# Layer 0's PSUM rings, two filters on TensorE, and placed transposes in a kernel of six stages

## The chip, the core and the metric

The kernel runs on one core of one Trainium2 chip, in one launch. The metric is the device time of that launch in microseconds: the median of several runs, lower is better. The profile is one further execution, taken by the hardware profiler, with a span of its own.

## What is computed

A batch of 8 images of 256 channels and 32 x 32 pixels goes through four layers; all numbers are fp32. The change touches the first layer, the feed-forward of the third, and the start of the fourth:

```python
# layer 0: attention of 4 heads, then a gated convolutional feed-forward
a = _attention(_ln(x, norm1_w, norm1_b), ...)     # _ln: x * rsqrt(mean(x*x)) * w + b
x = x + gamma1 * a
f = _edffn(_ln(x, norm2_w, norm2_b), ...)
x = x + gamma2 * f
# _attention: q, k, v by 1x1 convolution and batch norm; softmax(q k) v; plus a 3x3
#   depthwise convolution of v (pe); then a projection with batch norm (proj)
# _edffn: 1x1 convolution to 1024 channels (pi), 3x3 depthwise convolution,
#   gelu(first 512) * last 512, 1x1 convolution back (po), and in each 8x8 patch
#   a Fourier transform, a gain for each frequency, and the inverse
# layer 1: deformable convolution with group norms
# layer 2: causal attention with an MLP, then a feed-forward of the better half of the tokens
idx = top_k(x @ wr + br)[:, :511]; sel = x[idx]
y = (gelu(sel @ w1 + b1) @ w2 + b2) * weight[idx]
x = x + scatter(y, idx)
# layer 3: attention with squared scores on 8 heads, then a mixture of 8 experts
t = t + attention(layer_norm(t)); t = t + moe(layer_norm(t))
```

## The kernel before

The program is written in stages (`fast0`, `fast1`, `fast2`, `fast2f`, `fast3`, `fast3e`), each a Python generator that records instructions. Between two yields lies a piece of work. `by_time` (L1077) draws pieces from several such streams by their due times, so that pieces of different samples interleave. A scheduler then orders the instructions of each engine, within the data dependences, and may move one past its neighbours; `net.pinned` (L1037) keeps an instruction at the place in which it was recorded, relative to the other pinned ones of its engine. Every engine then executes its list strictly in order: an instruction that waits holds up all behind it. The tail of a stage overlaps the head of the next (`net.head`).

Tiles come from pools. A pool with n buffers hands them out in rotation, and a new tile waits until all readers of the one n places before it are done. [...]

**Layer 0** (`fast0`, L1094). The stream `attention` makes 128 steps: for each sample, each half of 512 queries (gq), and each of 8 key tiles (kt). A step makes the scores `s` of four heads (L1357, in two pairs of banks), their exponentials `e` on ScalarE (L1363), and, for the step before, sums of e on VectorE (L1319) and the products with v, which accumulate in `A` (L1323, one pair of banks of its own). After the eighth key tile `finish` normalises (D, rr, av, o) and projects (`proj`, L78, with the sum on VectorE in L1351). T = 32 ticks belong to one sample. Beside it run, each at due times of its own:

- `before_attention`: the norm (`ms`, `rb`, L1219), q, k and v (`qkv`), transposes of v (`vT`), the 3x3 convolution of v (`pe`, L1290).
- `before_gates` and `gates`: the second norm; for each of 8 groups of 128 channels the 1x1 convolution (`pi`, evacuated to `hp` in L1398), and then `depthwise`: the centre tap on ScalarE (L1223) and eight taps as one VectorE instruction each (L1230).
- `transforms`: `po`, the Fourier transform forward into the second bank of the same pair (L1455), the gain (L1456), the inverse (`back`, L1463), and the residual sum on VectorE (L1469).

All PSUM tiles but A come from one pool, `psS`, with three buffers of two banks: scores and all else take turns in it, and what needs one bank takes the first of a pair. When the 128 steps are recorded, `att.close()` frees the attention's space, and the rest of layer 0 goes on beside the head of layer 1.

**Layer 2's feed-forward** (`fast2f`, L2004). For each sample `before` ranks the tokens, `place` scatters the chosen ones to DRAM, `ready` loads them (xs), transposes them on TensorE (L2137) and copies them to `xk` on VectorE (L2138), `main` makes the two matrix products (h: L78, y: L2155), `after` gathers the results back (POOL) and adds them to the stream of tokens (L2182). T = 13 ticks belong to a sample.

**Layer 3** (`fast3`, L2457). `norm` loads a sample (SP's queue), normalises its tokens on VectorE (L1002, L1014), adds the output's bias to x on POOL (L2508), and transposes the result (L2514, copied in L2515).

Of the kernel before, what the change touches and what calls it, by code (L numbers as in the profile page):

```python
# [10 lines left out]
F32 = mybir.dt.float32  # L11
# [7 lines left out]
B = 8  # L19
# [1074 lines left out]
def fast0(net, io):  # L1094
# [3 lines left out]
    NT = N // P  # L1098
    yield HOLD
    with ExitStack() as ctx, ExitStack() as att:  # L1100
# [4 lines left out]
        psS = io.pool(ctx, "f0s", 3, PSUM)  # L1105
# [5 lines left out]
        psA = io.pool(att, "f0am", 1, PSUM)  # L1111
# [24 lines left out]
        def pair(name):  # L1136
            return psS.tile([P, 2, HF], F32, tag="S", name=name)

        def bank(name):
            return pair(name)[:, 0]  # L1140
# [51 lines left out]
        def sc(i):  # L1192
            return s[:, i : i + 1]
# [4 lines left out]
        def normed(xn, x, sq):  # L1198
# [13 lines left out]
            pr = pair("rb")  # L1212
            for h in range(2):
                nc.tensor.matmul(
                    pr[:, h], lhsT=net.unit[64 * h : 64 * h + 1, :], rhs=r[64 * h : 64 * h + 1, :],
                    start=True, stop=True,
                )
            pr = pr.rearrange("p h n -> p (h n)").unsqueeze(1).to_broadcast([P, KC, N])
            nc.vector.tensor_tensor(xn, x, pr, ALU.mult)  # L1219
# [13 lines left out]

        def before_attention(b):
# [6 lines left out]
            def projected(d, w, j, norm):  # L1241
                ps = pair("qkv")
                for h in range(2):
                    net.linear(ps[:, h], w, xn, bass.ts(j, P), bass.ts(h, HF))
                nc.scalar.activation(d, ps.rearrange("p h n -> p (h n)"), AF.Identity, scale=sc(norm), bias=sh(norm))
# [10 lines left out]
            for t4 in range(0, NT, 4):  # L1256
                ps = pair("vT")
                for i in range(4):
                    for c in range(KC):
                        lo = (i % 2) * C + c * P  # L1260
                        nc.tensor.transpose(ps[:, i // 2, lo : lo + P], v[:, c, bass.ts(t4 + i, P)], net.ident)
                nc.scalar.copy(
                    va[:, t4 : t4 + 4].rearrange("p t c d -> p (t c d)"), ps.rearrange("p h n -> p (h n)")
                )
                yield

            o = os[b] = atwo.tile([P, KC, N], F32, tag="o", name="o")
            for c in range(KC):
                ps = pair("pe")
                for h in range(2):  # L1270
# [12 lines left out]
                    yield  # L1283
                    for j, s_ in enumerate((0, -1, 1)):
                        for g in range(4):
                            to, fr = (
                                img(a)[:, :, max(0, -d_) : IMG - max(0, d_)]
                                for a, d_ in ((ps[32 * g : 32 * g + 32, h], s_), (thrice[:, g, :], -s_))
# [3 lines left out]
                            )  # L1292
                    yield
                nc.scalar.activation(
                    o[:, c, :], ps.rearrange("p h n -> p (h n)"), AF.Identity, scale=sc(4 + c), bias=sh(4 + c)
                )
                yield

        def attention():
# [31 lines left out]
            def finish(b, gq, A, total, x):  # L1331
# [16 lines left out]
                ps = pair("proj")  # L1348
                for c in range(KC):
                    net.linear(ps[:, c], wproj, o, bass.ts(c, P), cols)  # L1350
                    nc.vector.scalar_tensor_tensor(x[:, c], ps[:, c], sh(6 + c), x[:, c], ALU.add, ALU.add)  # L1351
                nc.sync.dma_start(out=mids[b][:, :, cols], in_=x)

            for i, (b, gq, kt) in enumerate(steps):
                ss = [pair("s") for _ in range(2)]
# [34 lines left out]
        def gates(b):  # L1390
            xn = xs.pop(b)

            def convolved(i):
                hp = two.tile([P, N], F32, tag="hp", name="hp")
                ps = pair("pi")
                for h in range(2):
                    net.linear(ps[:, h], wpi, xn, bass.ts(i, P), bass.ts(h, HF))
                nc.scalar.activation(hp, ps.rearrange("p h n -> p (h n)"), AF.Identity, bias=pib[:, i : i + 1])  # L1398
                a = cv[i] = five.tile([P, N], F32, tag="a", name="a")
                yield  # L1400
                yield from depthwise(img(a), img(hp), lambda t_: dw_taps[:, i, t_ : t_ + 1])
# [26 lines left out]
        def transforms(b):  # L1428
# [12 lines left out]
            for pr in range(4):  # L1441
# [3 lines left out]
                ps = pair("po")  # L1445
                for pc in range(2):
                    for k in range(4):
                        nc.tensor.matmul(
                            ps[:, 0, bass.ts(pc, C)], lhsT=hc[:, k, pc, :], rhs=wpo[:, k, :],
# [1715 lines left out]
```

## Time and profile before

| | us |
|---|---|
| median of 3 runs | 4487.3 |
| lowest and highest run | 4487.09, 4494.2 |
| the profiled execution | 4425.21 |
| its span, first to last instruction | 4423.1 |
| granted TensorE clock, mean | 0.953 |

By stretches of the span (busy us of each engine; the last column is the clock that TensorE was granted, as a share of full speed):

| stretch, us | what runs | PE | DVE | ACT | clock |
|---|---|---|---|---|---|
| 0 to 110.6 | layer 0 starts | 89.2 | 26.7 | 36.9 | 0.95 |
| 774.2 to 884.8 | layer 0, attention beside the feed-forward | 101.6 | 86.3 | 51.9 | 0.98 |
| 1327.2 to 1437.8 | layer 0 without attention, head of layer 1 | 79.5 | 94.5 | 41.0 | 0.87 |
| 1659.0 to 1769.6 | layer 1 | 102.1 | 87.7 | 71.7 | 1.00 |
| 2101.4 to 2212.0 | layer 2, attention | 108.5 | 31.7 | 43.0 | 1.00 |
| 2765.0 to 2875.6 | layer 2, feed-forward | 100.9 | 81.6 | 58.7 | 0.95 |
| 2875.6 to 2986.2 | its end and the start of layer 3 | 88.5 | 33.9 | 20.1 | 0.89 |
| 3428.6 to 3539.2 | layer 3, attention | 109.3 | 24.8 | 63.7 | 1.00 |
| 4202.8 to 4313.4 | layer 3, experts | 94.3 | 54.1 | 53.0 | 0.95 |

How to read profile rows in this text: a group has its line, engine and operation, then out<-in with shapes, then how often it ran, busy us and the mean ns of one, then the engine's idle time before it and who ended that. A wait is written as waiter <- releaser. A row of the timeline has a start, a duration, the instruction, how many of them, and in brackets the idle time before. TensorE shows two rows for one fp32 matmul, so x8 of pi are four matmuls. PE is TensorE's matmuls, PEld its weight loads, DVE VectorE, ACT ScalarE, POOL GpSimd, SP SyncE.

### The profile page before, as it was taken

How to read it: one execution, taken by the hardware profiler on the slowest of the kernel's cores; microseconds unless marked ns; L12 is line 12 of the kernel's file. 1: busy time of each engine (PE TensorE's matmuls, PEld its weight loads, DVE VectorE, ACT ScalarE, POOL GpSimd, SP SyncE). 2: the span in 40 equal slices, each digit the busy share in tenths (PEclk: the TensorE clock that was granted, in tenths of full speed). 3: DMA queues.
4: the chain of work that ended last, by engine and by line, in shares of the span. 5: the costliest groups of instructions: out<-in, count | busy, mean ns of one | idle time of the engine just before them, and what ended most of it. 6: DMA issues, size and time to landing. Idle time of an engine off the chain costs nothing. (4 is left out here: it accounts for less than half of the span.)

```text
span 4423.1 us, 52368 instructions
## 1 busy us (share of the span) xinstructions
PE 4007.3 (91%) x19836; PEld 1905.5 (43%) x19836; DVE 2321.2 (52%) x3976; ACT 2140.6 (48%) x2730; POOL 556.3 (13%) x633
## 2 busy tenths in 40 slices
PE   8989999999887889989999969988999999999887
PEld 3223333333333444444444436653333433336776
DVE  2387777777888677742222257732233223324345
ACT  3454445445443466633334355515555555566443
POOL 0000000000000000000000023420000000353753
PEclk9999999999998899999999979989999999999998
DMA  2212222222222111010001023371100000245667
GB/s 86 81 47 83 86 74 88 81 79 79 73 89 77 61 59 50 31 41 19 20 19 39 10 75 107 121 222 51 34 30 29 14 16 30 75 125 197 186 216 253
DMA packets 188423, 348.44 MB, mean 79 GB/s; under 512 B 23706, under 2 KB 132460, under 8 KB 176644
## 3 DMA queue, kind: packets, MB, share of 16 engines
q1 hardware_dynamic: 165396, 293.31, 20.5%
q0 software_dynamic: 19104, 46.45, 3.1%
q10 hardware_dynamic: 3664, 5.24, 0.3%
q8 instruction: 160, 2.62, 0.2%
q14 instruction: 99, 0.81, 0.1%
HBM read 174.24 MB, written 152.04 MB: 74 GB/s over the span
## 5 line engine op out<-in xcount | busy, mean ns | idle before, releaser
L1230 DVE SCALAR_TENSOR_TENSOR a<-hp,w_f_vec,a 128x992 f32<-128x992 f32 (+1 forms) x512 | 627.9, 1232 | 145.9 <-ACT a L1223 138.3
L2626 ACT ACTIVATE e<-s,five 128x1024 f32<-128x1024 f32 x512 | 539.5, 1109 | 280.5 <-PE s L2620 279.1
L2620 PE MATMUL s<-q,k 32*128 32x512 f32 x2048 | 371.2, 678 | 20.4 <-ACT e L2626 18.3
L1363 ACT ACTIVATE e<-s 128x1024 f32<-128x1024 f32 x256 | 249.6, 1019 | 228.7 <-PE s L1357 228.6
L2604 PE MATMUL A<-e,v 128*32 128x512 f32 x2048 | 297.3, 634 | 17.1 <-ACT e L2626 17.1
L1319 DVE TENSOR_TENSOR sum<-sum,e 128x1024 f32<-128x1024 f32 x192 | 230.8, 1220 | 114.8 <-ACT e L1363 114.8
L1323 PE MATMUL A<-e,va 128*32 128x512 f32 x2048 | 290.8, 605 | 0.0
L78 PE MATMUL pi<-xn,w_l_wpi 128*128 128x512 f32 x512 | 243.7, 619 | 36.7 <-ACT e L1363 20.0
L1357 PE MATMUL s<-q,k 32*128 32x512 f32 x1024 | 193.5, 642 | 12.8 <-DVE xn L1219 7.1
L2620 PEld LDWEIGHTS s<-q,k 32*128 32x128 f32 x2048 | 117.4, 192 | 201.5 <-issue 86.6
L1398 ACT ACTIVATE hp<-pi,pib 128x1024 f32<-128x1024 f32 x64 | 71.3, 1114 | 230.8 <-PE pi L78 222.5
L78 PEld LDWEIGHTS pi<-xn,w_l_wpi 128*128 128x128 f32 x512 | 96.0, 196 | 175.0 <-issue 108.6
L1681 PE MATMUL pos<-pos,w_f_sel 64*128 64x512 f32 x576 | 161.9, 627 | 7.7 <-ACT ay L1703 3.3
L2774 PE MATMUL h<-xk,w 128*128 128x128 f32 x1136 | 143.7, 281 | 20.4 <-DVE xk L2762 20.4
L1021 POOL DMA_INDIRECT res<-y,to x142 | 143.0, 1007 | 121.1 <-issue 84.7
L2745 ACT COPY w<-w_l3f_w 128x512 f32 x142 | 88.1, 623 | 143.2 <-PE h L2774 140.8
L2774 PEld LDWEIGHTS h<-xk,w 128*128 128x128 f32 x1136 | 140.4, 196 | 27.0 <-DVE xk L2762 20.4
L78 PE MATMUL h<-xk,w_l2f_w 128*128 128x512 f32 x256 | 124.3, 648 | 27.7 <-DVE xk L2138 27.7
L1274 POOL MEMSET thrice<- 32x128 f32 x32 | 6.3, 196 | 1109.7 <-PE pe L1290 1109.7
L1323 PEld LDWEIGHTS A<-e,va 128*32 128x32 f32 x2048 | 61.6, 110 | 194.1 <-issue 191.5
L2604 PEld LDWEIGHTS A<-e,v 128*32 128x32 f32 x2048 | 42.5, 110 | 236.6 <-issue 203.9
L1021 POOL DMA_INDIRECT so<-xl,rows x128 | 129.4, 1011 | 88.9 <-DMA xl<-mox 60.9
(396 smaller groups left out, 7031.0 us busy)
## 6 DMA issues: line engine op xcount, KB each, us to landing
x<-d SPq DMA_DIRECT2D x32, 1024.0 KB
xs<-so SPq DMA_DIRECT2D x70, 260.0 KB
so<-zero SPq DMA_DIRECT2D x5, 3380.0 KB
thrice<-v SPq DMA_DIRECT2D x256, 64.0 KB
gated<-st SPq DMA_DIRECT2D x32, 512.0 KB
hc<-gated SPq DMA_DIRECT2D x32, 512.0 KB
d<-x SPq DMA_DIRECT2D x16, 1024.0 KB
xl<-mox SPq DMA_DIRECT2D x64, 256.0 KB
```

The costliest lines, as they stand in the source:

```text
L78: self.nc.tensor.matmul(ps, lhsT=w[:, i, m], rhs=src[:, i, cols], start=(i == 0), stop=(i == k - 1))
L1021: made = self.nc.gpsimd.indirect_dma_start(**args)
L1230: nc.vector.scalar_tensor_tensor(to, fr, taps(t_), to, ALU.mult, ALU.add)
L1319: nc.vector.tensor_tensor(half, half, e[j], ALU.add)
L1323: nc.tensor.matmul(state["A"][32 * h : 32 * h + 32, c, :], lhsT=vas[b][:, kt, c, 32 * h : 32 * h + 32], rhs=e[h // 2][:, h % 2, :], start= ...
L1357: nc.tensor.matmul(ss[h // 2][:, h % 2], lhsT=ks[b][32 * h : 32 * h + 32, bass.ts(kt, P)], rhs=qs[b][32 * h : 32 * h + 32, bass.ts(gq, HF) ...
L1363: nc.scalar.activation(es[i][j], ss[j], AF.Exp, scale=SCALE)
L1681: nc.tensor.matmul(ps[:, bass.ts(h, HF)], lhsT=sel[r, t, xy, :], rhs=poss[b][r, :], start=True, stop=True)
L2604: nc.tensor.matmul(A[32 * h : 32 * h + 32], lhsT=v[:, kt, c * P + 32 * h : c * P + 32 * h + 32], rhs=e[:, h, :], start=first, stop=last,)
L2620: nc.tensor.matmul(ss[h // 2][:, h % 2], lhsT=k[32 * h : 32 * h + 32, c, bass.ts(kt, P)], rhs=q[32 * h : 32 * h + 32, c, bass.ts(hh, HF)], ...
L2626: nc.scalar.activation(e[:, 2 * j : 2 * j + 2], ss[j], AF.Square, scale=SCALE, bias=five)
L2774: nc.tensor.matmul(ps[:, j, m], lhsT=ws[j][:, k, bass.ts(m, P)], rhs=xk[:, j, k], start=(k == 0), stop=(k == KC - 1),)
```

## The change

1. **Layer 0, PSUM.** Scores get a pool of two pairs of their own. Everything else takes single banks from a pool of two ("X"). What was evacuated as one pair is now evacuated bank by bank (v, q, k, hp, vT, pe). The projection's result goes to av through ScalarE with its bias, and VectorE adds it to x from SBUF; `back` goes to u through ScalarE in the same way. The norm's product with rb is made in two halves. `finish` has one more yield before the projection.
2. **Layer 0, last sample.** Channel groups 1 and 7 are convolved by `by_products`: nine diagonal matrices made on ScalarE, and nine matmuls for each half image that accumulate in one bank, copied out by ScalarE. From the end of attention on, X is a pool of four banks.
3. **Layer 2, feed-forward.** The first transpose of xs of each sample, and the first matmul of each group of y, are pinned. `ready` is due at 8.8 instead of 9, with 1.9 instead of 2.2 between its pieces. For the last two samples the sums of `after` are due at T(b + 2) + 5 instead of + 1.2.
4. **Layer 3, norm.** The first sample is loaded by ScalarE's queue, the others by SP's as before. The bias on POOL is recorded after the transposes instead of before them.

```diff
-        psS = io.pool(ctx, "f0s", 3, PSUM)
+        own = {"X": io.pool(ctx, "f0x", 2, PSUM)}
...
-        psA = io.pool(att, "f0am", 1, PSUM)
+        psS, psA = io.pool(att, "f0s", 2, PSUM), io.pool(att, "f0am", 1, PSUM)
...
-        def pair(name):
-            return psS.tile([P, 2, HF], F32, tag="S", name=name)
-
         def bank(name):
-            return pair(name)[:, 0]
+            return own["X"].tile([P, HF], F32, tag="X", name=name)
...
-            pr = pair("rb")
             for h in range(2):
+                pr = bank("rb")
                 nc.tensor.matmul(
...
+                cols = bass.ts(h, HF)
+                nc.vector.tensor_tensor(
+                    xn[:, :, cols], x[:, :, cols], pr.unsqueeze(1).to_broadcast([P, KC, HF]), ALU.mult
+                )
...
+        def by_products(out, src, i):
+
+            diag = own["diag"].tile([P, 9, P], F32, tag="dg", name="dg")
+            for t_ in range(9):
+                nc.scalar.activation(diag[:, t_], net.ident, AF.Identity, scale=dw_taps[:, i, t_ : t_ + 1])
+            for h in range(2):
+                ps = bank("dw")
+                for n, t_ in enumerate((4, 0, 1, 2, 3, 5, 6, 7, 8)):
...
+                    nc.tensor.matmul(
+                        img(ps)[:, lo - HROWS * h : hi - HROWS * h, x0:x1], lhsT=diag[:, t_],
+                        rhs=img(src)[:, lo + dy : hi + dy, x0 + dx : x1 + dx], start=(n == 0), stop=(n == 8),
+                    )
+                    if n in (4, 8):
+                        yield
+                nc.scalar.copy(out[:, bass.ts(h, HF)], ps)
...
             def projected(d, w, j, norm):
-                ps = pair("qkv")
                 for h in range(2):
-                    net.linear(ps[:, h], w, xn, bass.ts(j, P), bass.ts(h, HF))
-                nc.scalar.activation(d, ps.rearrange("p h n -> p (h n)"), AF.Identity, scale=sc(norm), bias=sh(norm))
+                    ps = bank("qkv")
+                    net.linear(ps, w, xn, bass.ts(j, P), bass.ts(h, HF))
+                    nc.scalar.activation(d[:, bass.ts(h, HF)], ps, AF.Identity, scale=sc(norm), bias=sh(norm))
...
-                ps = pair("proj")
+                yield
                 for c in range(KC):
-                    net.linear(ps[:, c], wproj, o, bass.ts(c, P), cols)
-                    nc.vector.scalar_tensor_tensor(x[:, c], ps[:, c], sh(6 + c), x[:, c], ALU.add, ALU.add)
+                    ps = bank("proj")
+                    net.linear(ps, wproj, o, bass.ts(c, P), cols)
+                    nc.scalar.activation(av[:, c], ps, AF.Identity, bias=sh(6 + c))
+                nc.vector.tensor_tensor(x, x, av, ALU.add)
...
-                ss = [pair("s") for _ in range(2)]
+                ss = [psS.tile([P, 2, HF], F32, tag="S", name="s") for _ in range(2)]
...
-                yield from depthwise(img(a), img(hp), lambda t_: dw_taps[:, i, t_ : t_ + 1])
+                if b == B - 1 and i in BY_PRODUCTS:
+                    yield from by_products(a, hp, i)
+                else:
+                    yield from depthwise(img(a), img(hp), lambda t_: dw_taps[:, i, t_ : t_ + 1])
...
-                nc.tensor.matmul(ps[:, 1], lhsT=fwd, rhs=u.rearrange("p t c -> p (t c)"), start=True, stop=True)
+                ps = bank("fwd")
+                nc.tensor.matmul(ps, lhsT=fwd, rhs=u.rearrange("p t c -> p (t c)"), start=True, stop=True)
...
+                nc.scalar.copy(u.rearrange("p t c -> p (t c)"), back)
                 for c in range(KC):
                     xt = x[:, c, :].rearrange("p (h q w) -> p q h w", q=2, w=16)
-                    nc.vector.tensor_tensor(
-                        xt, back[:, 0, bass.ts(c, C)].rearrange("p (q h w) -> p q h w", q=2, w=16), xt, ALU.add
-                    )
+                    nc.vector.tensor_tensor(xt, u[:, c].rearrange("p (q h w) -> p q h w", q=2, w=16), xt, ALU.add)
...
         att.close()
+        own["X"], own["diag"] = io.pool(ctx, "f0t", 4, PSUM), io.pool(ctx, "f0d", 2)
...
-                    nc.tensor.transpose(ps[:, c * S + t * P : c * S + (t + 1) * P], xs[:, t, bass.ts(c, P)], net.ident)
+                    made = nc.tensor.transpose(
+                        ps[:, c * S + t * P : c * S + (t + 1) * P], xs[:, t, bass.ts(c, P)], net.ident
+                    )
+                    if c + t == 0:
+                        net.pinned(made)
...
-                        nc.tensor.matmul(
+                        made = nc.tensor.matmul(
                             ps[:, bass.ts(i, C)], lhsT=hid[:, k, bass.ts(t2 + i, P)], rhs=w2[:, k, :],
                             start=(k == 0), stop=(k == H // P - 1),
                         )
+                        if k == 0:
+                            net.pinned(made)
...
-                (T * (b - 1) + 9, 2.2, ready(b)), (T * b, 1, main(b) if b < B - 1 else last),
+                (T * (b - 1) + 8.8, 1.9, ready(b)), (T * b, 1, main(b) if b < B - 1 else last),
...
-            streams += [(T * (b + 1) + 7.6, 0.6, some(gathers, NT)), (T * (b + 2) + 1.2, 1, gathers)]
+            streams += [(T * (b + 1) + 7.6, 0.6, some(gathers, NT)), (T * (b + 2) + (1.2 if b < B - 2 else 5), 1, gathers)]
...
-            nc.sync.dma_start(out=halves(x), in_=tokens(io.src[b]))
+
+            (nc.sync if b else nc.scalar).dma_start(out=halves(x), in_=tokens(io.src[b]))
             yield
             xt = one.tile([P, NT, C], F32, tag="xt", name="xt")
             net.token_norm(xt, x, norms)
-            nc.gpsimd.tensor_tensor(x, x, bo.unsqueeze(1).to_broadcast([P, NT, C]), ALU.add)
             yield
...
+            nc.gpsimd.tensor_tensor(x, x, bo.unsqueeze(1).to_broadcast([P, NT, C]), ALU.add)
```

## The prediction

> **What bounds the kernel now.** I read the page first, then the waits of TensorE in layer 0, then busy times by stage, then the order of time at two seams. Rows of the page:
>
> ```profile
> span 4423.1 us, 52368 instructions
> ...
> PE 4007.3 (91%) x19836; PEld 1905.5 (43%) x19836; DVE 2321.2 (52%) x3976; ACT 2140.6 (48%) x2730; POOL 556.3 (13%) x633
> ...
> L1230 DVE SCALAR_TENSOR_TENSOR a<-hp,w_f_vec,a 128x992 f32<-128x992 f32 (+1 forms) x512 | 627.9, 1232 | 145.9 <-ACT a L1223 138.3
> ```
>
> TensorE is busy 91% of the span, so only what shortens its waits, or a stretch in which another engine rules, can move the end. The depthwise taps (L1230) are VectorE's largest group. From 221 to 1327 us (the attention loop of layer 0; ten windows of 110.6 us, added up) PE is busy 1005 of 1106 us, DVE 879, ACT 523. So PE leads, DVE follows at 79%, and ACT is half free. What PE waits for in layer 0 (us in total, times, longest):
>
> ```profile
> PE pi L78 <- ACT e L1363: 20.0, 18, 1.1
> PE proj L78 <- DVE x L1351: 15.8, 11, 2.5
> PE pi L78 <- DVE xn L1219: 13.4, 7, 2.3
> PE proj L78 <- DVE o L1346: 12.7, 3, 7.1
> PE qkv L78 <- DVE xc L1469: 9.3, 4, 2.3
> PE proj L78 <- ACT e L1363: 7.8, 7, 1.1
> ...
> PE s L1357 <- DVE xn L1219: 7.1, 5, 5.7
> ```
>
> Most of these are no data: pi does not use e, qkv does not use xc, s does not use xn. They are waits for a slot of the one ring of three bank pairs that scores and everything else share. The slot is held by an exponential, or by a sum on VectorE that stands behind depthwise taps of 1.23 us.
>
> After the loop VectorE rules. The stages (busy PE, PEld, DVE, ACT, POOL, then granted clock):
>
> ```profile
> 1420.00:1456.00 36.00, 6.66 (x26) 3.40 (x29) 35.87 (x45) 11.10 (x15) 0.00 (x0) 0.68 0.14 49
> ...
> 1302.00:1456.00 154.00, 96.70 (x318) 44.89 (x314) 128.96 (x146) 51.21 (x66) 6.01 (x6) 0.81 0.26 94
> ```
>
> At the end of layer 0 DVE is solid and PE waits 13.16, 7.97 and 4.87 us for layer 1's group statistics, queued on DVE among taps.
>
> Layer 2's feed-forward repeats this once per sample (start, duration, idle before):
>
> ```profile
> 2746.18 1.04 PE L2137 MATMUL xs<-ident,xs 128*128 128x128 f32 x8
> 2747.05 1.04 PE L2046 MATMUL xT<-ident,x 128*128 128x128 f32 x8
> 2750.82 15.39 PE L78 MATMUL h<-xk,w_l2f_w 128*128 128x512 f32 x32 [2.73 <-DVE xk L2138]
> ```
>
> and at the seam to layer 3 stand
>
> ```profile
> 2903.97 13.98 PE L2155 MATMUL y<-w_l2f_w,hid 128*128 128x256 f32 x64
> 2930.74 3.92 PE L2514 MATMUL xn<-ident,xt 128*128 128x128 f32 x16 [12.80 <-DVE xt L1014]
> 2934.70 1.13 PE L78 MATMUL qk<-xn,w_l_wq 128*128 128x512 f32 x2
> 2941.69 7.80 PE L78 MATMUL qk<-xn,w_l_wq 128*128 128x512 f32 x14 [5.86 <-DVE xn L2515]
> ```
>
> ```profile
> 2917.98 0.69 DVE L2160 TENSOR_TENSOR y<-y,w_f_b 128x512 f32<-128x512 f32 x1 [6.21 <-PE y L2155]
> ...
> 2926.05 0.75 DVE L1002 BATCH_NORM_STATS2 tn_s<-x 128x6 f32<-128x256 f32 x2 [6.55 <-DMA x<-d]
> ```
>
> **1. The rings of PSUM in layer 0.** Scores get two pairs of their own; all else gets two single banks, which ScalarE empties except for the normalising rows (rb) and the product with gain (fwd).
> Removed: waits for a slot held by ScalarE, 20.0 + 7.8 and four small rows (2.9, 2.2, 1.6, 1.1) = 35.6 us; held by VectorE, 15.8 + 9.3 + 7.1 and 1.5, 1.2, 0.5 = 35.4 us. The additional pause before proj gives the sums on DVE (o, 12.7) time: about 6 more. Together 77 us.
> Added on ACT: a 128x1024 eviction splits in two. Rows: hp 1.114 us for 1024 columns, hid (L2147) 0.687 for 512, so 0.26 us more for each of 128 splits, 33 us; 32 evictions of proj at 0.69 = 22; 32 of back at 0.585 (the row of u) = 19. These 74 us lift ACT from 47% to about 56% of the loop. [...]
> DVE: proj 32 x 0.747 becomes 16 x 1.22 (4.4 less), rb 16 x 2.28 becomes 32 x 1.22 (2.5 more): nothing.
> New waits: two banks turn about 448 times. In the built order, the PE work (from the trace's durations) between the last matmul into a bank and its next user is 1.9 us or more nearly everywhere, against 0.69 for an eviction plus at most 1.02 for an exponential ahead of it. The short ones: six times none (transposes of v right behind the mean square, which must wait for its logarithm: 0.69 and half an exponential, say 1.5 each, 9 us); five times 1.0 (2 us); fifteen behind rb, where DVE must multiply, 1.22 plus its queue. Most of those stand today as pi and qkv <- xn (13.4 + 4.7), so 4 us more. For the 60-odd places with 1.9, 0.2 each: 12. Together 27 us; behind a waiting matmul stand the next scores, so such a wait is paid in full. Bounds: 5 (only the certain ones) to 77 (0.17 per turn, nothing won). I take 27, since the distances nearly always exceed the eviction. **Net 50.**
>
> **2. Two depthwise filters of the last sample on TensorE.** DVE loses 16 taps x 1.23 = 19.7 us. PE gains 36 matmuls, two rows each, at 0.45 (pi x8 takes 3.60 us in this stretch), a little less at the edges: 31 us. ACT: 18 diagonals of 128x128 (hid L2780: 0.367) = 6.6 us. PE then has 97 + 31 = 128 us of work in 154, DVE 109. Bounds: 19.7 gained if PE hides everything; below, PE's 128 plus about 21 us of short waits that stay = 149, 5 gained. Second cost: on ACT's queue the diagonals stand before the loads of layer 1's weights, and PE already waits 4.9 us for one of those; up to 8 us more, taking 5 to -3. [...] **Net 10.**
>
> **3. Transposes in the feed-forward.** In the built order the eight xs transposes now stand before the last eight y matmuls (3.62 us) rather than directly before h. Today xk is ready 0.87 + 2.73 = 3.6 us after them, so the wait is just covered. Six waits (2.73 three times, 2.41, 2.55, 3.41) plus 0.57 = 17.1. Both xT groups now come before y, which covers most of the 0.2 to 0.5 us before wrow: 1. The first wait (10.6) stays. VectorE does xk at once, ahead of the ranking; the second y sum falls behind it, and the third h waits for its bank, some 1 us later than that sum ends, so nothing. Bounds: 9 to 19. **Net 18.**
>
> **4. The seam to layer 3.** The first x load goes to ACT's queue, behind the last gelu and a table load (ends 2906.2), instead of SP's, behind the store of y that waits until 2918.7. That load took up to 7.4 us then, so it lands near 2913. The statistics then wait for the last y sum, not for it: about 2919.8 instead of 2926.05 (6.2). The eight s sums (5.94 us) between the two xn copies go behind them: 5.86 shrinks to about 1 (5). The later sums and gathers wait on nobody near. The bias add stays first in POOL's order. Bounds 4 to 14. **Net 11.**
>
> **Sum.** 50 + 10 + 18 + 11 = 89. The profiled execution took 4425.2 us, so it would take 4336. The timed runs of before stand 1.4% above it; I take 89 from their median 4487.3: **4398**.
>
> **Rivals.**
> - *Two banks are too few, gain eaten* (part 1 nil): 39 gained, 4448. For: six turns with no work between. Against: the other distances.
> - *Two banks choke PE* (slower): every bank waits behind two exponentials. It decides above (77 + 39) / 448 = 0.26 us per turn; at 0.4 it costs 179, so 4487 - 116 + 179 = 4550. For: ACT serves scores and banks in one order. Against: exponentials are 2 us in steps of about 10.
> - *The tail becomes TensorE's*: part 2 loses 6, 4414. For: 128 of 154.
> - *xk comes no earlier in time* although it stands earlier: part 3 nil, 4416. Against: DVE waits for wrow just then.
> - *More falls than the slots*: the remaining waits on xn, u and o (some 30 us) go too, 4368.
>
> **Numbers.** Chances: forecast 0.62, too few 0.12, tail 0.09, xk 0.04, more 0.09, choke 0.04. All low ends of 1 to 4 together gain 0 - 3 + 9 + 4 = 10 us (4477), all high ends 72 + 20 + 19 + 14 = 125 (4362); all low ends at once are unlikely, so the range is 4355 to 4452, which takes in every rival but the slower one. 0.2% is about what this measurement can tell: faster 0.95, same 0.01, slower 0.04.
>
> **What would show it.** pi and proj no longer wait for e or x of DVE, and PE's share in the loop rises above 94%; vT waits for the logarithm; 16 fewer taps and PE over 125 us busy between loop and layer 1; h without 2.7 us waits; xn at the seam waits about 6.6 us, qk about 1. Wrong if PE gets new waits on bank evictions of over 50 us, or if DVE in the loop goes above 90%.

## The result, and the profile after

| | before | after |
|---|---|---|
| median of 6 runs, us | 4487.6 | 4449.5 |
| lowest and highest | 4470.8, 4499.7 | 4440.6, 4465.0 |
| ratio, 95% interval | | 0.9919 [0.9892, 0.9946] |
| the profiled execution, us | 4425.2 | 4449.3 |

The change gains 38 us where 89 were forecast. The two profiled executions can't be subtracted from one another: that of before took less time than any of its timed runs (4471 us and more), that of after is like its own. A second profile of before, taken later, serves below where stages are compared.

The page of the changed kernel begins with its span, then busy time, share and instructions by engine. The third row is the group of the depthwise taps:

```profile
span 4447.6 us, 52740 instructions
...
PE 4051.6 (91%) x19908; PEld 1944.8 (44%) x19908; DVE 2297.9 (52%) x3960; ACT 2219.1 (50%) x2942; POOL 556.3 (13%) x633
...
L1230 DVE SCALAR_TENSOR_TENSOR a<-hp,w_f_vec,a 128x961 f32<-128x961 f32 (+1 forms) x496 | 608.5, 1232 | 155.1 <-ACT a L1223 147.0
```

There are 16 taps fewer, as counted, and ScalarE has 78 us more (the prediction's two terms make 81). What TensorE waits for in layer 0 (from 0 to 1440 us; us in total, times, longest):

```profile
PE pi L78 <- DVE u L1480: 31.0, 8, 5.0
PE ms L1204 <- ACT sq L1202: 19.2, 9, 6.1
PE fwd L1479 <- DVE xn L1217: 18.1, 4, 4.5
PE c L1595 <- DMA w_l_w<-in_l_w_dram: 11.3, 1, 11.3
PE pi L78 <- DVE xn L1217: 8.8, 4, 7.8
```

The slot waits on e, x and xc are gone, but for 0.4 us on e. In their place stand waits on the two kinds of bank that VectorE empties: the product with gain (u, out of the bank of fwd) and the normalising rows (xn, out of rb). They are fewer, and most are four to five microseconds long where most of the old ones were one or two. The row of ms is another matter, to which step 1 below comes back.

Between the loop and layer 1, the window that the prediction showed for before, has now (busy PE, PEld, DVE, ACT, POOL, then granted clock):

```profile
1302.00:1456.00 154.00, 122.09 (x360) 56.09 (x362) 98.95 (x118) 57.34 (x95) 6.01 (x6) 0.83 0.29 104
```

VectorE has 30 us less to do there (20 are the taps; the rest falls before this window, since the loop ended earlier) and TensorE 25 more, but the point at which layer 1's second set of offsets starts (L1620) has not moved: 1455.5 us, against 1456.0 before, though the loop ended 12 us earlier (the last A at 1289 instead of 1301 us).

In the feed-forward the products h follow the copies without a wait, and wrow waits now and then; at the seam xn waits 9.0 us instead of 12.8, qk not at all, and two new waits stand behind it:

```profile
2708.49 13.90 PE L78 MATMUL h<-xk,w_l2f_w 128*128 128x512 f32 x32
2737.91 1.48 PE L2107 MATMUL wrow<-ident,wcol 128*128 128x128 f32 x8 [3.41 <-DVE wcol L2102]
...
2932.17 4.02 PE L2544 MATMUL xn<-ident,xt 128*128 128x128 f32 x16 [9.04 <-DVE xt L1014]
2962.12 1.09 PE L2576 MATMUL kT<-ident,k 128*128 128x128 f32 x8 [3.70 <-DVE v L2564]
2966.65 5.66 PE L2587 MATMUL G<-kt 128*128 128x129 f32 x32 [3.44 <-DVE kt L2580]
```

### The profile page after: what moved, and what is told of

The parts are those of the page before. It is cut to its first block, busy times and chain, and to the rows that moved or that the text cites. A ratio compares the mean times of both kernels' runs of the same rounds, so it can differ in the third digit from the quotient of the medians.

```text
span 4447.6 us, 52740 instructions
## 1 busy us (share of the span) xinstructions
PE 4051.6 (91%) x19908; PEld 1944.8 (44%) x19908; DVE 2297.9 (52%) x3960; ACT 2219.1 (50%) x2942; POOL 556.3 (13%) x633
## 5 line engine op out<-in xcount | busy, mean ns | idle before, releaser
L1230 DVE SCALAR_TENSOR_TENSOR a<-hp,w_f_vec,a 128x961 f32<-128x961 f32 (+1 forms) x496 | 608.5, 1232 | 155.1 <-ACT a L1223 147.0
L78 PE MATMUL pi<-xn,w_l_wpi 128*128 128x512 f32 x512 | 268.9, 672 | 41.5 <-DVE u L1480 31.0
L1341 PE MATMUL A<-e,va 128*32 128x512 f32 x2048 | 268.5, 605 | 0.0
L2805 PE MATMUL h<-xk,w 128*128 128x128 f32 x1136 | 153.7, 293 | 57.6 <-DVE xk L2793 48.6
L1418 ACT ACTIVATE hp<-pi,pib 128x512 f32<-128x512 f32 x128 | 87.7, 688 | 230.0 <-PE pi L78 223.9
L78 PEld LDWEIGHTS pi<-xn,w_l_wpi 128*128 128x128 f32 x512 | 104.9, 215 | 199.2 <-issue 119.4
L2640 DVE TENSOR_TENSOR o<-A,r 128x512 f32<-128x512 f32 x32 | 22.1, 690 | 228.5 <-PE A L2635 228.5
L2827 PE MATMUL y<-w_l3f_w,hid 128*128 x568 | 137.1, 384 | 0.0
```

Of the source, the lines that this page charges most:

```text
L78: self.nc.tensor.matmul(ps, lhsT=w[:, i, m], rhs=src[:, i, cols], start=(i == 0), stop=(i == k - 1))
L1230: nc.vector.scalar_tensor_tensor(to, fr, taps(t_), to, ALU.mult, ALU.add)
L1341: nc.tensor.matmul(state["A"][32 * h : 32 * h + 32, c, :], lhsT=vas[b][:, kt, c, 32 * h : 32 * h + 32], rhs=e[h // 2][:, h % 2, :], start= ...
L2805: nc.tensor.matmul(ps[:, j, m], lhsT=ws[j][:, k, bass.ts(m, P)], rhs=xk[:, j, k], start=(k == 0), stop=(k == KC - 1),)
L2827: nc.tensor.matmul(ps[:, j, :], lhsT=hid[:, j, k, :], rhs=w[:, k, :], start=(k == 0), stop=(k == KC - 1))
```

## The experiments

Each group of runs shared a chip with runs of the kernel before, and is compared with those: their median was 4480 us for e1 to e4 and 4482 for e9 to e12 (the slower chips), and 4419 for e5 to e8 and for e13 to e15 (the quicker ones). These medians differ by more than the change is worth, so only the differences on one chip, or ratios, are used.

**e1: the kernel before, profiled again.** No edit.

> The kernel before once more, for a profile taken on the same chip as the variants. Theory A (long waits of TensorE lower its clock, so the changed kernel's loop runs slower for the same work): the attention loop of layer 0 shows a granted clock of 0.95 or more and ends (last A) near 1301 us, as in the first profile, against 0.92 in the changed kernel. Rival B (the first profile was only a quick execution): the loop shows 0.92 to 0.93 and ends 10 to 15 us later, near 1315, and the span is near 4470 to 4480 us.

Measured: 4480.0 us, span 4470.0. Theory A holds for the loop: layer 0 is the same as in the first profile, to 4 us (last A at 1298.0), with a granted clock of 0.95 to 0.99. Of rival B only the span came true, and not by the loop. The quick part of the first profile lies behind it: from the first h to the last y of the feed-forward 276.7 us there, 313.6 here. The waits of TensorE of e1 from 2640 to 2945 us show where:

```profile
PE wrow L2083 <- DVE wcol L2078: 34.6, 6, 9.2
PE h L78 <- DVE xk L2138: 12.9, 7, 2.7
```

In the first profile wrow waited 1.9 us in this window. So the prediction's view of this stage was not that of the slower chips.

**e2: part 1 alone.** All hunks of layer 0, none of `fast2f` and `fast3`, and

```diff
-                if b == B - 1 and i in BY_PRODUCTS:
+                if False:
```

> Part 1 alone: the rings in layer 0, no filters on TensorE, the rest as before. The forecast's step: 50 us gained. Theory A (the banks that VectorE empties, fwd and rb, hold TensorE for about 60 us and their length lowers its clock): 10 to 20 us gained, pi waits for u some 30 us in all with single waits of 4 to 5 us. Rival C (ScalarE's 74 us of added evictions are on the path): no gain or a loss, and TensorE waits for hp, o or va copies by 30 us or more.

Measured: 4456.8 us, ratio 0.9947 [0.9934, 0.9960], 23.5 us gained instead of 50. From 221 to 1217 us of the loop, first e1, then e2 (columns as above):

```profile
221.00:1217.00 996.00, 911.48 (x4450) 335.31 (x4446) 784.72 (x727) 480.36 (x513) 4.53 (x23) 0.98 0.25 77
```

```profile
221.00:1217.00 996.00, 917.20 (x4513) 346.48 (x4514) 798.30 (x739) 538.28 (x661) 4.51 (x23) 0.93 0.25 78
```

The clock fell from 0.98 to 0.93. The waits of e2 in that window:

```profile
PE pi L78 <- DVE u L1480: 23.9, 6, 5.0
PE fwd L1479 <- DVE xn L1217: 18.1, 4, 4.5
PE ms L1204 <- ACT sq L1202: 17.9, 7, 6.6
PE pi L78 <- DVE xn L1217: 9.8, 7, 7.8
PE back L1487 <- DVE u L1480: 3.0, 1, 3.0
```

Of the waits for copies that rival C asked for there are 4.3 us (hp 2.6, o 1.7), far from its 30. That favours theory A, which e7 and e8 test by taking the cause away.

**e3: part 3 alone** (the hunks of `fast2f`, but for the late sums of the last two samples).

> Part 3 alone: the pinned transposes and the earlier selection in layer 2's feed-forward, the rest as before. The forecast's step: 18 us gained. Rival (what h no longer waits for, wrow and y wait for instead): 0 to 5 us gained, with wrow waiting 16 us in all where it waited 6.

Measured: 4452.4 us, ratio 0.9930 [0.9918, 0.9942], 27.8 us gained, more than the forecast's 18. The rival fell: wrow waits 5.5 us in all, h 3.8, and what is new is smaller (y 10.0 where e1 had 4.0, without a cause that the trace names; xs 6.0 for its load). From the first h to the last y it takes 285.0 us, 28.6 less than e1.

**e4: part 4 alone.**

```diff
-            nc.sync.dma_start(out=halves(x), in_=tokens(io.src[b]))
+            (nc.sync if b else nc.scalar).dma_start(out=halves(x), in_=tokens(io.src[b]))
...
-            nc.gpsimd.tensor_tensor(x, x, bo.unsqueeze(1).to_broadcast([P, NT, C]), ALU.add)
...
+            nc.gpsimd.tensor_tensor(x, x, bo.unsqueeze(1).to_broadcast([P, NT, C]), ALU.add)
...
-            streams += [(T * (b + 1) + 7.6, 0.6, some(gathers, NT)), (T * (b + 2) + 1.2, 1, gathers)]
+            streams += [(T * (b + 1) + 7.6, 0.6, some(gathers, NT)), (T * (b + 2) + (1.2 if b < B - 2 else 5), 1, gathers)]
```

> Part 4 alone: the first load of layer 3 on ScalarE's queue and the late s sums of the last two samples, the rest as before. The forecast's step: 11 us gained. Rival (the moved s sums collide with the copies of v and kt, and kT and G wait for those): 3 us gained, no measurable difference.

Measured: 4473.8 us, ratio 0.9984 [0.9975, 0.9994]: 6.4 us gained, by the interval 3 to 11. Between the two. The collision is there: kT waits 2.3 us for v and G 2.8 for kt (0.8 in e1), which takes back half of what xn (9.9 instead of 12.9) and qk (none instead of 5.2) give. Why xn gave 3 us and not 6 stands in VectorE's order and, in the last row, ScalarE's:

```profile
2951.30 0.17 DVE L1003 BATCH_NORM_AGGREGATE tn_m<-tn_s 128x2 f32<-128x6 f32 x1
2954.85 0.43 DVE L1002 BATCH_NORM_STATS2 tn_s<-x 128x6 f32<-128x256 f32 x1 [3.37 <-DMA x<-d]
2955.19 0.17 DVE L1003 BATCH_NORM_AGGREGATE tn_m<-tn_s 128x2 f32<-128x6 f32 x1
2955.39 0.30 ACT L1004 ACTIVATE tn_r<-tn_m,eps 128x8 f32<-128x8 f32 x1 [20.34 <-DVE tn_m L1003]
```

The first sample's eight statistics began soon after the last sum of y (2948.29, the sum ended at 2947.56), as forecast. But ahead of their eighth aggregate (2955.19), for which ScalarE waits, stands the ninth statistic, which is the second sample's. That sample's load is still on SP's queue, behind the store of y, and VectorE waits 3.4 us for it.

**e5 to e8: the changed kernel, and what is taken out of it.** e6 has `if False:` as above. e7 empties the bank of fwd by a ScalarE copy, and e8 that of rb too, without the filters:

```diff
-                nc.vector.tensor_tensor(
-                    u, ps.rearrange("p (t c) -> p t c", c=C), gain.unsqueeze(1).to_broadcast([P, 2, C]), ALU.mult
-                )
+                nc.scalar.copy(u.rearrange("p t c -> p (t c)"), ps)
+                nc.vector.tensor_tensor(u, u, gain.unsqueeze(1).to_broadcast([P, 2, C]), ALU.mult)
...
+                rs = s_[:, cols]
+                nc.scalar.copy(rs, pr)
                 nc.vector.tensor_tensor(
-                    xn[:, :, cols], x[:, :, cols], pr.unsqueeze(1).to_broadcast([P, KC, HF]), ALU.mult
+                    xn[:, :, cols], x[:, :, cols], rs.unsqueeze(1).to_broadcast([P, KC, HF]), ALU.mult
                 )
```

(s_ is the tile of squares, which nothing reads any more by then.)

> The changed kernel once more, on the same chip as the next three. If the parts add up (23.5 for the rings, 27.8 for the feed-forward, 6.4 for the seam, as measured one by one), and the filters on TensorE bring the forecast's 10 us, it stands 68 us below the kernel before; if the filters lose 14 us, as the distance between the rings' run and the changed kernel from the loop's end to layer 1 says, 44 us.

> The changed kernel without part 2: all depthwise taps of the last sample stay on VectorE, the rest is unchanged. The forecast's step: 10 us slower than the changed kernel. Theory D (the tail of layer 0 is TensorE's, its 33 us of filter matmuls are on the path): 10 to 15 us faster than the changed kernel, and layer 1's second set of offsets starts earlier by as much after the loop's end.

> The changed kernel with the fwd bank emptied by a ScalarE copy (0.59 us), and the product with gain made by VectorE from SBUF; everything else as changed. Theory A (the bank that waits for VectorE holds TensorE): pi's waits for u, 31 us in 8 waits of 4 to 5 us, are gone, the granted clock in the loop rises from 0.93 to 0.95 or more, and it is 25 to 40 us faster than the changed kernel. Rival C (ScalarE is what holds the banks): no faster, since ScalarE gets 32 copies more, 19 us. Rival E (VectorE itself is late, and the next user of u waits instead): the waits move to back, which needs the product, and it is within 5 us of the changed kernel.

> The changed kernel without part 2 and with both banks that VectorE empties, fwd and rb, copied out by ScalarE first. If theories A and D hold: the 31 us of fwd, some 15 to 25 us of rb (fwd and pi waiting for xn), and the 10 to 15 us of part 2, together 50 to 70 us faster than the changed kernel. If rival C holds: at most the 10 to 15 us of part 2.

| run | median, us | below before, us | ratio, 95% |
|---|---|---|---|
| e5 changed kernel | 4386.5 | 32.6 | 0.9929 [0.9914, 0.9944] |
| e6 without filters | 4371.8 | 47.3 | 0.9897 [0.9881, 0.9913] |
| e7 fwd by ScalarE | 4352.9 | 66.2 | 0.9860 [0.9842, 0.9877] |
| e8 fwd and rb by ScalarE, no filters | 4314.0 | 105.1 | 0.9766 [0.9751, 0.9781] |

The filters cost 14.7 us (e5 to e6): theory D, and the opposite of the forecast's step. The copy of fwd gains 33.6 us (e5 to e7), that of rb another 24.2, if the three gains add (e8, less the other two: 72.5 - 33.6 - 14.7). Theory A holds, and C and E fall: 58 us are bought by more work on ScalarE, which is still busy only 60% of the loop. The same window of e8, and its waits:

```profile
221.00:1217.00 996.00, 951.46 (x4835) 362.99 (x4838) 861.46 (x800) 600.15 (x752) 4.51 (x23) 0.97 0.26 83
```

```profile
PE ms L1204 <- ACT sq L1202: 16.6, 7, 5.5
PE pi L78 <- ACT u L1482: 5.5, 6, 1.5
PE back L1488 <- DVE u L1483: 4.9, 2, 2.9
PE qkv L78 <- DVE xn L1219: 3.3, 1, 3.3
```

The copy out of fwd takes 0.59 us, and the waits for it make 5.5 us in all, where those for VectorE made 23.9. e7 fell short in one point: its clock in this window rose to 0.94 only, not 0.95. The long waits of fwd for rb's reader (18.1 us) were still there; e8, without them, has 0.97. e8 is faster than both kernels.

**e9 and e10: one filter each.** `BY_PRODUCTS` is `(1,)`, then `(7,)`.

> The changed kernel with only the first of the two filters (chunk 1) on TensorE, the second (chunk 7) back on VectorE. Without both it was 14.7 us faster than with both. Theory D1 (both filters load a stretch that is TensorE's anyway): half of it, about 7 us faster than the changed kernel. Theory D2 (the second one costs, since its 17.9 us stand in one piece before layer 1's first matmuls of the second sample): 14 us faster. Theory D3 (the first one costs): no faster.

> The changed kernel with only the second filter (chunk 7) on TensorE, the first (chunk 1) back on VectorE. D1: about 7 us faster than the changed kernel. D2: no faster. D3: 14 us faster.

Measured: 4435.7 us, 0.9879 [0.9854, 0.9905], and 4432.5 us, 0.9885 [0.9863, 0.9907]. e5 and e6 ran on another chip, so the comparison is made over the stretch that the filters can touch, from the last A to layer 2's first qk: 650.0 us with both (e5), 639.2 with the first alone, 641.1 with the second alone, 632.9 with none (e6). By these single profiles each costs 6 to 11 us, and none is free: D1.

**e11 and e13: the halves of part 3.** e11 has the pins without the new due times, e13 this alone:

```diff
-                (T * (b - 1) + 9, 2.2, ready(b)), (T * b, 1, main(b) if b < B - 1 else last),
+                (T * (b - 1) + 8.8, 1.9, ready(b)), (T * b, 1, main(b) if b < B - 1 else last),
```

> The kernel before with the pins of part 3 alone (xs and y take their planned place in TensorE's order), without the earlier stream of the selection. If the pins make the gain of part 3 (27.8 us): 24 to 30 us below the kernel before. If the earlier selection makes it, since wrow waited 34.6 us for its columns in the profile of the kernel before on this chip: under 10 us below, and wrow still waits 20 us or more.

> The kernel before with the other half of part 3 alone: the stream that scatters, reads and transposes the selected rows (xs) is due 0.2 earlier and at a denser pace (8.8 and 1.9 in place of 9 and 2.2), no pins. The pins alone brought nothing (4480.8 against 4481.5 us). Theory G (the earlier stream is the whole of part 3): 25 to 30 us below the kernel before, wrow waits 10 us or less in all. Theory H (only both together work): under 5 us below.

Measured: 4480.8 us, 0.9999 [0.9987, 1.0012] for the pins, 4398.7 us, 0.9953 [0.9937, 0.9968] for the due times, 20.7 us gained: theory G in the main, though it asked for 25. The pins are inert by themselves: in e11 the xs transposes stand where they stood, behind y and ahead of xT and h, and wrow waits as in e1. In e13 they stand ahead of the last y matmuls, and h waits only once, for the first sample. That wrow is short in e13 proves little, since e13 ran on a quicker chip and wrow was short in the first profile of before too; that the change shortens it is shown by e3 against e1 (5.5 and 34.6 us). The waits of e11, of e13, and a sample of e13 in order of time:

```profile
PE wrow L2083 <- DVE wcol L2078: 40.4, 7, 9.3
...
PE h L78 <- DVE xk L2142: 10.7, 6, 2.7
```

```profile
PE h L78 <- DVE xk L2138: 11.6, 1, 11.6
...
PE wrow L2083 <- DVE wcol L2078: 4.4, 3, 3.9
```

```profile
2722.14 1.07 PE L2137 MATMUL xs<-ident,xs 128*128 128x128 f32 x8 [0.49 <-DMA xs<-so]
2723.04 3.62 PE L2155 MATMUL y<-w_l2f_w,hid 128*128 128x256 f32 x16
2726.50 13.90 PE L78 MATMUL h<-xk,w_l2f_w 128*128 128x512 f32 x32
```

The 3.62 us of y between xs and h hide the copy to xk.

**e12: part 2 alone**, in the kernel before with its bank pairs.

> Part 2 alone: the kernel before with its three bank pairs, and the two filters on TensorE. The forecast's step: 10 us gained. Theory D: 10 to 15 us lost, as in the changed kernel. Rival F (the filters lose only where the rings have let TensorE arrive earlier): 0 to 10 us gained.

Measured: 4500.4 us, 1.0040 [1.0026, 1.0053], 18.9 us lost. Rival F falls: the filters lose without the rings too. From the last A to layer 1's second set of offsets, first e1, then e12:

```profile
1298.00:1452.00 154.00, 96.84 (x316) 44.88 (x309) 129.23 (x146) 51.52 (x66) 6.01 (x6) 0.81 0.26 94
```

```profile
1298.00:1473.00 175.00, 133.94 (x394) 61.07 (x386) 111.50 (x130) 56.14 (x85) 6.01 (x6) 0.84 0.24 84
```

TensorE gets 37 us more, VectorE loses 18, and TensorE's idle time falls by 16 only (57 to 41). How the second filter joins the chain instead of filling a gap is seen in the order of time, first of e1, then of e12 (TensorE, and two rows of VectorE):

```profile
1437.98 0.59 PE L1548 MATMUL gn_m<-gn_mv,w_f_gsel 128*128 128x1 f32 x2 [13.16 <-DVE gn_mv L1545]
...
1451.99 6.49 PE L1596 MATMUL off<-xpad,w_f_woff 64*32 64x512 f32 x34 [4.86 <-DVE xpad L1582]
```

```profile
1452.05 17.43 PE L1247 MATMUL dw<-hp,dg 128*128 128x512 f32 x36 [10.60 <-ACT hp L1419]
1469.31 0.28 PE L1573 MATMUL gn_m<-gn_mv,w_f_gsel 128*128 128x1 f32 x2
...
1473.47 6.18 PE L1621 MATMUL off<-xpad,w_f_woff 64*32 64x512 f32 x36 [2.67 <-DVE xpad L1607]
```

```profile
1452.68 0.17 DVE L1570 BATCH_NORM_AGGREGATE gn_mv<-gn_st 128x2 f32<-128x6 f32 x1
...
1469.63 0.16 DVE L1576 COPY gn_t<-gn_m 128x1 f32<-128x1 f32 x1 [14.23 <-PE gn_m L1573]
```

The filter waits for its input hp, then runs 17.4 us. The statistics of layer 1 (gn_mv) are ready 0.8 us after its start, but their product gn_m stands behind it in TensorE's order, and VectorE waits 14.2 us for that. Before, the same stretch of TensorE's order was a wait of 13.2 us for these statistics, which VectorE made among the taps. One wait went, a longer piece of work came. It accounts for the smaller part of the loss: the statistics themselves come 15 us later than in e1 (1452.9 against 1437.9), after the first filter, which TensorE does in one piece of 15.1 us at 1378.64. From them to the offsets it is 6.5 us more (20.6 against 14.1).

**e14 and e15: the gathers of the feed-forward later.**

```diff
-            streams += [(T * (b + 1) + 7.6, 0.6, some(gathers, NT)), (T * (b + 2) + 1.2, 1, gathers)]
+            streams += [(T * (b + 1) + 13.6, 0.6, some(gathers, NT)), (T * (b + 2) + 6.6, 1, gathers)]
```

> The kernel before with GpSimd's gathers of yg in layer 2's feed-forward due 6 units later, so that five of a sample's eight stand between the scatters of the next sample and no burst has twelve indirect DMAs; their sums on VectorE are due 5.4 later. In the profile of the kernel before on this chip, five sums of y started 0.7 to 2.2 us after the end of such a burst, 7.5 to 8.9 us late. Theory I (the burst holds up TensorE's and VectorE's hand-over): these waits shrink below 4 us each and the kernel is 15 to 30 us faster than before. Theory J (the burst only happens to end there): no faster, or slower by the later sums.

> The changed kernel without the filters, with fwd and rb copied out by ScalarE (105 us below the kernel before in the run with both), and with the later gathers as well. If theory I holds: 115 to 130 us below the kernel before. If theory J holds: 100 us or less below.

Measured: 4443.1 us, 1.0066 [1.0044, 1.0088], and 4353.7 us, 0.9859 [0.9835, 0.9882] (65.6 below before): both some 24 to 40 us worse than without this edit. The later sums waited for their rows: in e14 VectorE waited 36.5 us, in 20 waits, for the gathered rows yg. The sums of y waited 8.5 us in all, less than in e1, but that says nothing. The five late sums were seen in e1, on a slower chip; e14 and e15 ran on one of the quicker, and no profile of the kernel before was taken there. So the expectation's "on this chip" is not so, and the runs do not tell theories I and J apart.

## Why the prediction was wrong, by its own steps

**1. The rings (net 50; 23.5 measured): a mis-sized term.** That the slot waits on e, x and xc go was right. The term that failed is the one for the new waits: 27 us in the prediction, about 67 in e2 (from 221 us to the last A, where some 73 us of e1's waits went): "for the 60-odd places with 1.9, 0.2 each" and "4 us more" behind rb. It priced nearly every turn of the two banks by ScalarE's copy of 0.69 us. Two kinds of turn are VectorE's, and VectorE's price is not the 0.68 us of its product but the taps queued in front of it. At the end of the loop, in VectorE's and then in TensorE's order of time of the changed kernel:

```profile
1287.37 7.58 DVE L1230 SCALAR_TENSOR_TENSOR a<-hp,w_f_vec,a 128x961 f32<-128x961 f32 x6
1294.86 0.68 DVE L1480 TENSOR_TENSOR u<-fwd,w_l_gam 128x512 f32<-128x512 f32 x1
```

```profile
1290.09 1.12 PE L1479 MATMUL fwd<-u,w_l_fwd 128*128 128x512 f32 x2
1291.05 1.89 PE L78 MATMUL pi<-xn,w_l_wpi 128*128 128x512 f32 x4
1295.60 1.98 PE L78 MATMUL pi<-xn,w_l_wpi 128*128 128x512 f32 x4 [2.66 <-DVE u L1480]
```

The bank of fwd is filled by 1291.2 and read at 1294.86, after six taps. With two banks, the first pi takes the other, and the second stands still. In the kernel before the ring had three places, one more between a bank and its next user. In the window above these waits make 54.8 us in e2 (23.9 + 18.1 + 9.8 + 3.0), where e1 had 13.4 (pi for xn), and they have a second price: their length. In e2 two groups of the same eight matmuls, one behind such a wait:

```profile
426.05 6.69 PE L78 MATMUL pi<-xn,w_l_wpi 128*128 128x512 f32 x8 [3.77 <-DVE u L1480]
...
449.21 3.70 PE L78 MATMUL pi<-xn,w_l_wpi 128*128 128x512 f32 x8
```

Behind the wait of 3.8 us the eight matmuls take another 3.0 us. The prediction charged the waits of part 1 with their own length alone. What the profiles show beside them is the granted clock, which they record as either full or half (1.0 or 0.5 in each of the 250 records of the first two profiles). In the loops of e1, e2, e7 and e8 half clock followed each of the 22 waits of 3.8 us and more (it began at most 3.5 us after the wait's end). But it also followed 31 of the 56 waits between 1.2 and 3.3 us, and 3 of the 74 shorter ones, so these traces, in which the ends of matmuls are modelled, show no length below which it never followed. Added up over the loop (221 us to the last A):

| | loop ends, us | waits of 3.8 us and more | at half clock, us | mean row of pi, ns |
|---|---|---|---|---|
| e1 before | 1298.0 | 2 | 51 | 616 |
| e2 rings | 1280.4 | 13 | 137 | 676 |
| e7 fwd by ScalarE | 1254.3 | 6 | 123 | 636 |
| e8 fwd and rb by ScalarE | 1217.6 | 1 | 58 | 605 |

TensorE was busy in 48 of e1's 51 us at half clock, and in 116 of e2's 137. Half of the difference, 34 us, is an estimate of the matmul time that the clock cost e2; it takes matmuls at half clock to last twice as long, as the eight above nearly did (6.69 and 3.70 us).

With both banks emptied by ScalarE (e8), layer 0's loop is 80 us shorter than in e1, so there was that much to be had. That this is near the prediction's 77 us of waits is in part luck. From the start to the last A, the same 5748 rows of TensorE took (us):

| | in all | TensorE idle | busy | A, 2048 rows | pi, 432 | proj, 120 |
|---|---|---|---|---|---|---|
| e1 before | 1298.0 | 121.0 | 1177.0 | 291.0 | 204.1 | 64.7 |
| e2 rings | 1280.4 | 105.7 | 1174.7 | 267.8 | 228.4 | 55.1 |
| e8 fwd and rb by ScalarE | 1217.6 | 68.6 | 1149.0 | 265.9 | 200.2 | 56.0 |

Of the 80 us only 52 are waits; 28 are busy time. In e2 pi, which stands behind most of the long waits, takes 24 us more, and A takes 23 less, though one row of A lasts as long in both (606 and 605 ns): its rows overlap more. TensorE stood still for over 0.25 us 78 times in e1, 42 in e2 and 45 in e8, so a short wait probably costs something beside its own length too; no run separates this. The prediction had neither effect, and in e2 they nearly cancel.

The prediction's own falsifier, "new waits on bank evictions of over 50 us", is met only if pi's waits for xn are counted as new; its sign of 94% TensorE in the loop did not come (92.1% in e2; 95.5% in e8). VectorE stayed at 80%, far from the other falsifier of 90%. The sum charged nothing for ScalarE's 74 us of added evictions, and that held: from 221 to 1217 us of e2 TensorE waits 4.3 us for ScalarE's copies (hp 2.6, o 1.7), with ScalarE busy 538 of 996 us. vT hardly waits at all. The long wait before the norm is that of the mean square for its squares (ms on sq, 17.9 us in the loop of e2, 3.0 in e1), and it is no wait for a bank: in all seven cases ScalarE had itself waited 1.5 to 6.7 us for the load of the norm's input (xn) before it made the square. It is still there in e8 (16.6 us).

**2. The filters (net 10; a loss of 15 to 19 measured): wrong in sign.** The step that failed is "PE's 128 plus about 21 us of short waits that stay". TensorE's work came out at 134 us, and 41 us of waits stayed (e12). They stay because the stretch is no contest of two engines' sums but a chain through both (layer 1's product, its statistics, its offsets), and the filters were put into the chain in TensorE's order. The lower bound of 5 assumed that TensorE's sum is the floor. The other fear, that weight loads behind the diagonals would be late, is not the cause: c waits 11.1 us for them in e2, which has no diagonals, and 11.3 in the changed kernel. This was the rival "the tail becomes TensorE's", two to three times as dear as it was priced. The row of pi put the two filters at 31 us, some 15 each, and the second took 17.0 to 17.9 in the runs that have it. So the row was a fair measure of a filter's price, and the sum around it was what failed.

**3. The feed-forward (net 18; 20.7 to 27.8 measured): right in mechanism.** The xs transposes stand ahead of the last y matmuls, and the waits of h on xk go. e11 and e13 show that the due times of the stream put them there, not the pins. The gain is well above the forecast on the slower chip, where wrow waits 35 us in the kernel before, which the quick first profile did not show. The rival "xk comes no earlier" fell.

**4. The seam (net 11; 6.4 measured): mis-sized, by two steps.** xn gained 3.0 us in e4 (3.8 in the changed kernel) instead of 6.2. "The statistics then wait for the last y sum, not for it" held for their start, but the load of the second sample, which still stands behind the store of y on SP's queue, holds up the last of them by 3.4 us: the prediction moved one load and did not ask what the next one would stop. qk gained its whole wait, but the sums that were moved behind xn meet v and kt: the last eight wait for their gathered rows one by one, the copies of v and kt stand behind them, and kT and G wait 3.7 and 3.4 us for these in the changed kernel. "The later sums and gathers wait on nobody near" is what failed here: nobody waited for the sums to end, but two copies waited behind them.

**The sum.** 23.5 - 14.7 + 27.8 + 6.4 = 43, or 39 with the loss of e12; the changed kernel gained 38 beside its own runs of before, and 33 on e5's chip, where the sum is 36 if part 3 brings what e13 showed on the other quicker chip, 20.7. Nothing of weight is left over. The time that came is the one that the rival "two banks are too few" named (4448), by luck, for its road was another: it had part 1 at nothing and part 2 at a gain. Two banks were enough for what ScalarE empties, not for what VectorE does.

Not separated by a run of its own: what the length of the waits costs apart from the waits. e7 and e8 remove both at once.

## What to carry to other kernels

Before tiles are put into one short ring, list for each kind who empties it; price a turn by what is queued ahead of the reader on its engine, not by the reader's own time, and let the engine with the short queue copy the tile out, even if that adds work. Count waits by length too: one of 3.8 us cost another 3.0 in the matmuls behind it here, while half clock followed only 3 of 74 waits of under 1.2 us. Before a load is moved to another queue, look which load comes next for the same reader. Work taken from a busy engine fills another's idle time only if its place in that engine's order has nothing behind it that ends the stage; otherwise it is added to the chain (e12 lost 18.9 us here).

## What was not expected of the hardware

Two executions of one program differ in part of it only. The kernel before took 4480 us on two of the chips and 4419 on the two others (each chip served one group of runs, so the chip and the hour are not told apart), and the profiles differ almost only where GpSimd issues indirect DMAs. The changed kernel's first profile is 59 us longer than that of e5. Both reach the first h at 2634 us; the feed-forward, from there to the last y, took 287.8 us in the one and 249.9 in the other, and the rest of the difference comes in the experts of layer 3, between 4000 and 4200 us, where the other indirect DMAs are.

In the profiles with the longer feed-forward VectorE stood still there until GpSimd's burst of twelve indirect DMAs was over, in this order of time of e1 (first GpSimd's last issue of a burst, then VectorE):

```profile
2739.28 0.95 POOL L2172 DMA_INDIRECT yg<-pk,idx  x1 [0.30 <-issue]
```

```profile
2740.93 0.69 DVE L2160 TENSOR_TENSOR y<-y,w_f_b 128x512 f32<-128x512 f32 x1 [7.46 <-remote]
```

The matmuls whose sum this is stand in the trace as ended at 2732.8; VectorE began 8 us later, 0.7 us after the burst's end. Five sums of e1 look so, and none of the first profile, with bursts of the same length. What passes between the two is not settled: e14 broke up the bursts, but on a quicker chip and with a new wait of its own.
